# Emptying finished PSUM groups with ScalarE copies instead of VectorE adds in a four-layer attention kernel

## The chip, the cores and the metric

The kernel runs on one core of one Trainium2 chip. The time is the device time of one launch in microseconds (us), the median of several runs. The profile is one execution of the same program, recorded by the hardware profiler; its engines are called PE (TensorE's matmuls), PEld (TensorE's weight loads), DVE (VectorE), ACT (ScalarE), POOL (GpSimd) and SP (SyncE).

## What is computed

The input `x` is 4 images of 64 x 64 positions with 64 channels, fp32. Four layers follow one another:

- layer 0: self-attention over the 4096 positions of an image, `x = gamma * out + x`
- layer 1: layer norm, a 1x1 product to 256 channels, a depthwise 3x3 convolution, a gate, a 1x1 product back; then a second gated pair of 1x1 products; each added to `x`
- layer 2: attention without weights, in which the same memory is read as `B, C, H, W`
- layer 3: attention with 32 channels, a 1x1 product, then a normalization over all four images, added to `x`

What matters here is layer 2. In the reference it is

```
scores = jnp.einsum('bci,bcj->bij', xf, xf)
attn = jax.nn.softmax(scores, axis=-1)
out = jnp.einsum('bcj,bij->bci', xf, attn).reshape(B, C, H, W)
return out + x
```

with 4096 x 4096 scores per image. Because they are symmetric, the kernel computes only a part of the blocks and uses some exponentials twice, once as they are and once transposed.

## The kernel before, in words

**Order of the work.** Everything is unrolled at build time into a list of items; the instruction order on PE, ACT, DVE and POOL is the program's own order (`manual_schedule`), and each engine works through its own queue in that order. Only SP's queue (DMAs) is ordered by the tool. An item of layer 0 is a tile of 128 rows, one of layer 2 a block of 256 keys against 512 queries, one of layer 3 a tile of 128 keys. All images go through layer 0 first (items of image 0, 1, 2, 3), then layer 2 of image 0, then for each later image its layer 2 followed by layer 3 of the image before it, and last the layer 3 of image 3. Smaller work is woven in by two lanes, `conv` (layer 1 of an image, written as a generator that says how many nominal microseconds each step takes) and `misc` (projections, transposed inputs), which are advanced by `tick` in each item. `conv` carries layer 1 of image 3 during layer 2 of image 0. That puts the depthwise convolution (L1240 and L1243 on DVE, its first tap L1236 on ACT for image 3) and the writes of its padded input (L1222 on ACT, from the 1x1 products L1205) between the instructions of image 0's layer 2. `features2` (L1307 on PE, L1310 half on DVE and half on ACT) makes the transposed input `ko` of image 1 in the same stretch, in the `misc` lane.

**Layer 2 of one image.** A list of steps `(h, g, u, run, ti)` is built: `h` is one of 8 groups of 512 queries, `g` and `u` choose 256 keys. `item(n)` issues, in this order, the scores of step n (`score`, L1380, 8 matmuls into one of three 1024-wide PSUM slots, then two exps of 128x512, L1385, into an `e` tile), for mirrored steps the transposition of the exps (`turned`, L1398 on DVE) and their column sums (`column_sums`, L1413 by DMA for image 0, L1415 on POOL for the others, L1417 at the end of a group), then in image 0 a piece of `conv` and of `misc`, and last the products of the step two before (`products`, L1439, 8 matmuls). Products of one group accumulate in two PSUM banks, 6 and 7 (`new_acc`), one per row half `r`; each is a 128x512 tile. There is one such pair, so the first product of the next group can't start before both banks have been read. Image 0's groups are worked in the order 0, 1, 2, 3, 4, 7, 6, 5 (108 steps), the others' in the order 7, 0, 1, ..., 6 (72 steps).

**The sum array.** The result of a group, and what the transposed exps add to other groups, is gathered in an SBUF tile `m.A` (128x4096, 512 columns per group). It is allocated at step 2 of the image and cleared by POOL (L1478). At a group's last product two DVE adds (L1431, through `add_to`) add the two banks to its columns. `turned_products` (L1456, 128 small matmuls, 3.64 us) makes the contribution of a pair of mirrored blocks in two PSUM slots, and four adds of 128x256 (L1431 too) put it into the columns of the two groups of the pair. `spread_sums` (L1425 and L1426 on DVE) turns a group's column sums once POOL has finished them; for the last mirrored group it is issued after item `len(items) + 3` (image 0) or `+ 1` (the others). `close2` reads `m.A` and the sums (L1507, L1527) in the next image's items: its first part comes at item 8.

**Buffers.** `e` tiles (128x2048) come from a pool of six (`new_e`); a pair of steps shares one. In image 0 one of the six holds `xr`, the weights of the turned products, and one at a time holds `esum`. `A` comes from a pool of five large tiles.

Of the kernel before, what the change touches and what calls it, by code (L numbers as in the profile page):

```python
# [691 lines left out]
def fast_path(ctx: ExitStack, tc: tile.TileContext, a: dict, out: bass.AP, bad):  # L692
    nc = tc.nc
# [19 lines left out]
    PS = pp.tile([128, 4096], F32, name="PS")  # L713
# [12 lines left out]
    def new_ps():  # L726
        if turn_of["banks"]:
            if turn_of["bank"] % turn_of["banks"] == turn_of["banks"] - 1:
                turn_of["bank"] += 1
            k = new_bank(), new_bank()  # L730
            return PS[:, 512 * k[0] : 512 * k[0] + 1024]
        s = turn_of["slots"][turn_of["ps"] % len(turn_of["slots"])]
        turn_of["ps"] += 1
        return PS[:, bass.ts(s, 1024)]
# [9 lines left out]
    def new_acc():  # L744
        turn_of["acc"] += 1
        return PS[:, bass.ts(6 + turn_of["acc"] % 2, 512)]

    def new_e(name="e"):
        return ep.tile([128, 2048], F32, tag="e", name=name)
# [4 lines left out]
    def new_big(name):  # L754
        return big.tile([128, 4096], F32, tag="big", name=name)
# [78 lines left out]
    for nm in names128:  # L834
        r = flat[nm].shape[0] // 128
# [154 lines left out]
    items, due = [], {}  # L990

    def at(i, fn):
        due.setdefault(i, []).append(fn)
# [87 lines left out]
    def follow(lag=LAG):  # L1081
        if len(late) > lag:
            late.pop(0)()
# [238 lines left out]
    def layer2(b, when_free=None):  # L1322


        x, m, first = X[:, b], im[b], len(items)
# [14 lines left out]
        m.mirrored = [h for h, _ in (PART if b == 0 else FULL) if mine_t[h]]  # L1340
        spread_at = {mine_t[h][-1] + 5: h for h in m.mirrored}
        late_start, tiles = (6, 1) if b == 0 else (4, 2)
        used, todo = {}, []
        st = {"e": {}, "T": {}, "esum": {}}

        def slot(g, t):
# [4 lines left out]
        def weights(h):  # L1351
            if "xr" not in st:
                st["xr"] = new_e("xr") if b == 0 else xn.tile([128, 2048], F32, tag="xn", name="xn")
            for q in range(4):
                for k in range(4):
                    c = 1024 * (h % 2) + 256 * k
                    nc.sync.dma_start(  # L1357
                        out=st["xr"][32 * q : 32 * q + 32, c : c + 256],
                        in_=x[32 * k : 32 * k + 32, 256 * h : 256 * h + 256],
                    )  # L1360
# [6 lines left out]
        def score(n):  # L1367
            h, g, u, _, _ = steps[n]
            if n == 0:
                if b:  # L1370
                    take_slots(0, 1, 2)
                m.zs = sm.tile([128, 216], F32, tag="zs2", name="zs2")
            if n % 2 == 0:
                st["pair"] = new_e()
            e = st["e"][n] = st["pair"][:, bass.ts(n % 2, 1024)]
            ps = new_ps()
            for r, c in quads:
                rows_ = slice(64 * r, 64 * r + 64)
                k = 512 * g + 256 * u + 128 * r + 64 * c
                mm(  # L1380
                    ps[64 * c : 64 * c + 64, bass.ts(r, 512)], m.ko[rows_, k : k + 64],
                    m.ko[rows_, bass.ts(h, 512)], start=True, stop=True,
                )
            for r in range(2):
                act(  # L1385
                    e[:, bass.ts(r, 512)], ps[:, bass.ts(r, 512)], AF.Exp, bias=SHIFT2,
                    accum_out=slot(g, 2 * u + r),
                )

        def turned(n):  # L1390
            _, _, _, run, ti = steps[n]
            if run is None:
                return
            k = run % tiles
            if k not in st["T"]:
                st["T"][k] = new_big("turned")
            T = st["T"][k].rearrange("p (e s j) -> p s e j", e=16, s=8)
            nc.vector.transpose(  # L1398
                T[:, 2 * ti : 2 * ti + 2], st["e"][n].rearrange("p (s e i) -> p s e i", s=2, e=16)
            )  # L1400

        def column_sums(n):
            h, _, _, run, _ = steps[n]
            if run is None:
                return
            k, e = mine_t[h].index(n), st["e"][n]
            if k == (0 if b == 0 else 1):
                st["esum"][h] = new_e("esum")
            if h not in st["esum"]:
                return  # L1410
            esum = st["esum"][h][:, 0:1024]
            if b == 0:
                nc.gpsimd.dma_start(out=esum, in_=e, **({} if k == 0 else {"accum_op": ALU.add}))  # L1413
            else:
                nc.gpsimd.tensor_add(esum, st["e"][mine_t[h][0]] if k == 1 else esum, e)  # L1415
            if n == mine_t[h][-1]:
                nc.gpsimd.tensor_add(esum[:, 0:512], esum[:, 0:512], esum[:, 512:1024])  # L1417

        def spread_sums(h):
            if h == m.mirrored[0]:  # L1420
                m.cs = sm.tile([128, 128], F32, tag="cs2", name="cs2", bufs=1)
                if b == 0:
                    nc.gpsimd.memset(m.cs, 0.0)
            esum = st["esum"][h]
            nc.vector.transpose(esum[:, 512:1024], esum[:, 0:512])  # L1425
            nc.vector.tensor_reduce(  # L1426
                m.cs[:, bass.ts(h, 16)], esum[:, 512:1024].rearrange("p (e j) -> p e j", j=32), AX.X, ALU.add
            )

        def add_to(cols, ps):  # L1430
            nc.vector.tensor_add(cols, ps, cols)  # L1431

        def products(n):
            h, g, u, _, _ = steps[n]
            if n == mine[h][0]:
                st["acc"] = new_acc(), new_acc()
            for r, c in quads:
                rows_ = slice(64 * r, 64 * r + 64)
                mm(  # L1439
                    st["acc"][r][64 * c : 64 * c + 64, :], xw[rows_, 4 * g + 2 * u + c, :],  # L1440
                    st["e"][n][rows_, bass.ts(c, 512)], start=n == mine[h][0], stop=n == mine[h][-1],
                )
            if n == mine[h][-1]:
                for r in range(2):
                    add_to(m.A[:, bass.ts(h, 512)], st["acc"][r])

        def turned_products(run):
            h, pair, _ = runs[run]
            T, slots = st["T"][run % tiles], [new_ps(), new_ps()]
            for e in range(16):  # L1450
                c = e % 2
                w = 1024 * (h % 2) + 256 * (e % 4) + 64 * (e // 4)
                for q in range(4):
                    rows_ = slice(32 * q, 32 * q + 32)
                    o = 512 * (q % 2)
                    mm(  # L1456
                        slots[q // 2][64 * c : 64 * c + 64, o : o + 256], st["xr"][rows_, w : w + 64],
                        T[rows_, bass.ts(e, 256)], start=e < 2, stop=e >= 14,
                    )
            view = m.A.rearrange("p (g t q j) -> p g q t j", g=8, t=4, q=4)  # L1460
            for i in range(2):
                for gi, g in enumerate(pair):
                    add_to(
                        view[:, g, 2 * i : 2 * i + 2],
                        slots[i].rearrange("p (q m) -> p q m", q=2)[:, :, 128 * gi : 128 * gi + 128]
                        .rearrange("p q (t j) -> p q t j", j=32),
                    )

        def item(n):
            if n in weights_at:  # L1470
                weights(weights_at[n])
            score(n)
            turned(n)
            column_sums(n)
            todo.append(n)
            if n == 2:
                m.A = new_big("A")
                nc.gpsimd.memset(m.A, 0.0)  # L1478
            if b == 0:
                follow(0)  # L1480
                conv.tick(2.9)
                misc.tick(1.8)
            if n >= late_start:
                for _ in range(2):
                    if todo and todo[0] <= n - 2:
                        products(todo.pop(0))
            for run, (_, _, last) in enumerate(runs):
                if n - 2 == last:
                    turned_products(run)
                    if run == len(runs) - 2 and when_free:  # L1490
                        when_free()
            if n in spread_at:
                spread_sums(spread_at[n])

        for n in range(len(steps)):
            items.append((lambda n=n: item(n), 1.6 if b else 0.0))
        at(len(items), lambda: [products(todo.pop(0)) for _ in range(2)])
        for n, h in spread_at.items():
            if n >= len(steps):
                at(len(items) + (1 if b else 3), lambda h=h: spread_sums(h))  # L1500

    def close2(b):
        x, m = X[:, b], im[b]
# [525 lines left out]
```

## Time and profile before

| | |
|---|---|
| three runs | 2481.69, 2482.59, 2482.92 us; median 2482.59 |
| the profiled execution | 2481.6 us, of it 2479.7 between its first and last instruction (the span) |
| TensorE busy | 2428.8 us, 98% of the span |
| ScalarE busy | 1651.6 us, 67% |
| VectorE busy | 1466.9 us, 59% |
| GpSimd busy | 534.1 us, 22% |
| mean granted TensorE clock | 0.995 |
| layer 2 of image 0 | about 1019 to 1284 us from the span's start |
| layer 2 of images 1, 2, 3 | from about 1283, 1620 and 1957 us |
| group ends on VectorE (L1431, 128x512) | 64 adds, 686 ns mean |
| turned contributions (L1431, 128x256) | 188 adds, 417 ns mean |
| clearing of A (L1478, GpSimd) | 4, at 1023.5, 1292.1, 1608.6 and 1944.4 us, 3.5 to 3.8 us each |

A row of the profile's tables names a line of the code, the engine, the operation, and `out<-in` with the tile names; a time line row begins with its start and length in us and ends, in brackets, with the idle time of its engine before it and what ended it. A row with `xN` merges N neighbouring instructions. A row of the waits names engine, tile and line that waited, then `<-` what it waited for, the total in us, the number of times and the longest. A row of the windows gives a stretch, its length, then busy time (and instructions) of PE, PEld, DVE, ACT and POOL, the clock granted to TensorE (1.00 is full), the share of DMA time and GB/s.

### The profile page before, as it was taken

The page shows a single profiled execution, that of the slowest core. Times are in us where ns is not written, and L with a number is a line of the kernel's source. Part 1 is how long each engine was busy: PE and PEld are TensorE (multiplying, and loading weights), DVE is VectorE, ACT ScalarE, POOL GpSimd, SP SyncE. Part 2 cuts the span into 40 slices and gives each one's busy share as a digit, 9 for nine tenths or more (in the row PEclk, how much of TensorE's full clock was granted, in tenths as well). Part 3 has the DMA queues.
Part 4 walks back from the last instruction along what each step waited for, and adds up shares of the span by engine and source line. Part 5 has one row for each costly group of instructions (what it writes and reads, how often), then busy time and mean ns, then how long its engine had stood idle before and what let it go on. Part 6 is the DMA issues. An engine that isn't in the chain of part 4 may idle for free.

```text
span 2479.7 us, 63372 instructions
## 1 busy us (share of the span) xinstructions
PE 2428.8 (98%) x27381; PEld 932.6 (38%) x27381; DVE 1466.9 (59%) x1778; ACT 1651.6 (67%) x3162; POOL 534.1 (22%) x374
## 2 busy tenths in 40 slices
PE   9999999999999999989999999999999999999997
PEld 3343453336433633344334442134431244421113
DVE  2010377227822782377446657877668876678886
ACT  4666766676666666667744449954479754579996
POOL 2000000000000000100026662247631365622110
PEclk9999999999999999999999999999999999999999
DMA  3000000000000000320240017610065400296554
GB/s 79 1 18 1 18 1 18 18 19 1 18 18 18 1 18 18 65 48 18 52 86 19 19 45 154 135 29 19 19 130 121 92 19 19 61 173 141 120 118 117
DMA packets 65172, 129.57 MB, mean 52 GB/s; under 512 B 12556, under 2 KB 33269, under 8 KB 64885
## 3 DMA queue, kind: packets, MB, share of 16 engines
q0 software_dynamic: 22592, 80.26, 16.2%
q1 hardware_dynamic: 41541, 43.33, 7.7%
q8 instruction: 217, 3.56, 0.6%
q10 hardware_dynamic: 752, 1.85, 0.2%
q14 instruction: 70, 0.57, 0.1%
HBM read 4.80 MB, written 4.19 MB: 4 GB/s over the span
## 4 chain that ended last, share of the span: by engine, by line
PE 87%; DVE 6%; ACT 4%; issue 1%; SPq 1%; DMA 0%; POOL 0%; DVEq 0%; ACTq 0%
PE PS L1121 17%; PE PS L1095 17%; PE PS L1380 10%; PE PS L1439 10%; PE PS L1612 9%; PE PS L1673 8%; PE PS L1456 7%; DVE tg L1664 2%; PE PS L1205 2%; ACT e L1623 1%; DVE y L1240 1%; ACT e L1385 1%; SPq L1357 1%; ACT e L1100 1%; PE PS L1170 1%
## 5 line engine op out<-in xcount | busy, mean ns | idle before, releaser
L1100 ACT ACTIVATE e<-PS 128x1024 f32<-128x1024 f32 x512 | 524.2, 1024 | 333.1 <-PE PS L1095 300.1
L1385 ACT ACTIVATE e<-PS 128x512 f32<-128x512 f32 x648 | 380.7, 595 | 380.2 <-PE PS L1380 361.7
L1121 PE MATMUL PS<-e,vq 64*64 64x512 f32 x4096 | 577.2, 592 | 0.0
L1095 PE MATMUL PS<-X,q 64*64 64x512 f32 x4096 | 575.1, 591 | 1.8 <-DVE X L979 1.7
L1623 ACT ACTIVATE e<-PS 128x512 f32<-128x512 f32 (+2 forms) x588 | 500.4, 921 | 60.8 <-PE PS L1612 40.1
L1664 DVE TENSOR_TENSOR tg<-tg,e 128x2048 f32<-128x2048 f32 x172 | 393.9, 2290 | 42.6 <-ACT e L1623 31.0
L1439 PE MATMUL PS<-e,X 64*64 64x512 f32 x2592 | 373.6, 597 | 16.5 <-DVE A L1431 15.7
L1380 PE MATMUL PS<-ko 64*64 64x512 f32 x2592 | 376.1, 600 | 2.2 <-DVE A L1431 1.5
L1240 DVE SCALAR_TENSOR_TENSOR y<-pad,vec,y 128x1024 f32<-128x1024 f32 x240 | 308.0, 1283 | 29.8 <-ACT y L1236 22.4
L1415 POOL TENSOR_TENSOR esum<-esum,e 128x1024 f32<-128x1024 f32 x126 | 298.8, 2371 | 58.2 <-ACT e L1385 51.3
L1612 PE MATMUL PS<-tg,ph 32*64 32x512 f32 x4096 | 296.8, 612 | 2.6 <-DVE A L1431 1.8
L1398 DVE STREAM_TRANSPOSE turned<-e 128x1024 f32<-128x1024 f32 x188 | 231.4, 1239 | 112.5 <-ACT e L1385 112.5
L1095 PEld LDWEIGHTS PS<-X,q 64*64 64x64 f32 x4096 | 184.1, 133 | 258.8 <-issue 178.6
L1121 PEld LDWEIGHTS PS<-e,vq 64*64 64x64 f32 x4096 | 184.1, 133 | 252.2 <-issue 157.2
L1673 PE MATMUL PS<-e,tg 128*32 128x512 f32 x2048 | 272.5, 604 | 0.0
L1478 POOL MEMSET A<- 128x4096 f32 x4 | 14.7, 3675 | 1006.8 <-PE PS L1121 1006.8
L1439 PEld LDWEIGHTS PS<-e,X 64*64 64x64 f32 x2592 | 111.9, 134 | 198.9 <-issue 166.4
L1108 DVE TENSOR_REDUCE sums<-zs 128x1 f32<-128x4 f32 x128 | 19.7, 154 | 270.0 <-ACT e L1100 269.7
L1431 DVE TENSOR_TENSOR A<-PS,A 128x256 f32<-128x256 f32 (+1 forms) x252 | 110.5, 486 | 112.2 <-PE PS L1456 91.2
L1380 PEld LDWEIGHTS PS<-ko 64*64 64x64 f32 x2592 | 105.5, 133 | 167.4 <-issue 142.2
L1645 POOL DMA_DIRECT2D xn<-e x116 | 101.1, 898 | 291.2 <-ACT e L1623 208.0
L1456 PE MATMUL PS<-turned,xn 32*64 32x256 f32 x5376 | 157.9, 377 | 2.3 <-DVE sums L1519 1.4
(213 smaller groups left out, 1630.4 us busy)
## 6 DMA issues: line engine op xcount, KB each, us to landing
xn<-e POOLq DMA_DIRECT2D x132, 512.0 KB, 5.4
xn<-X SPq DMA_DIRECT2D x336, 32.0 KB
esum<-e POOLq DMA_DIRECT2D x20, 512.0 KB, 4.9
xn<-t SPq DMA_DIRECT2D x64, 128.0 KB
ph<-tg SPq DMA_DIRECT2D x64, 128.0 KB
ko<-ko SPq DMA_DIRECT2D x32, 128.0 KB
xr<-in_x_dram SPq DMA_DIRECT2D x13, 256.0 KB
q<-q SPq DMA_DIRECT2D x12, 256.0 KB
```

What stands on the lines that cost most here:

```text
L1095: mm(ps[64 * c : 64 * c + 64, bass.ts(r, 512)], m.q[rows_, 128 * t + 64 * c : 128 * t + 64 * c + 64], x[rows_, bass.ts(g, 512)], start=Tru ...
L1100: act(es[g // 2][:, bass.ts(g % 2, 1024)], ps, AF.Exp, bias=SHIFT0, accum_out=zs[:, g : g + 1],)
L1121: ins = mm(PS[64 * s : 64 * s + 64, 2048 + 512 * j : 2560 + 512 * j], vq[rows_, :], es[j // 2][rows_, k : k + 512], start=t == 0 and i < 2 ...
L1240: stt(y1, win, wt, y1, ALU.mult, ALU.add)
L1380: mm(ps[64 * c : 64 * c + 64, bass.ts(r, 512)], m.ko[rows_, k : k + 64], m.ko[rows_, bass.ts(h, 512)], start=True, stop=True,)
L1385: act(e[:, bass.ts(r, 512)], ps[:, bass.ts(r, 512)], AF.Exp, bias=SHIFT2, accum_out=slot(g, 2 * u + r),)
L1439: mm(st["acc"][r][64 * c : 64 * c + 64, :], xw[rows_, 4 * g + 2 * u + c, :], st["e"][n][rows_, bass.ts(c, 512)], start=n == mine[h][0], st ...
L1456: mm(slots[q // 2][64 * c : 64 * c + 64, o : o + 256], st["xr"][rows_, w : w + 64], T[rows_, bass.ts(e, 256)], start=e < 2, stop=e >= 14,)
L1612: mm(PS[64 * c : 64 * c + 64, bass.ts(banks[k], 512)], m.ph[32 * k : 32 * k + 32, 128 * mc + 64 * c : 128 * mc + 64 * c + 64], m.th[32 * k ...
L1623: act(e[:, 512 * lo : 512 * k], PS[:, 512 * banks[lo] : 512 * banks[lo] + 512 * (k - lo)], AF.Exp,)
L1664: nc.vector.tensor_add(esum, esum, e)
L1673: mm(st["y"][32 * k : 32 * k + 32, :], m.gx[:, i % 32, :], es[i][:, bass.ts(k, 512)], start=mc == 0, stop=i % 32 == 31,)
```

## The change

`add_to` is gone. A set `seen` records, for each image and while the program is built, which groups already have a contribution in `A`.

- At a group's end, if its columns have nothing yet, ScalarE copies the first bank (128x512) into them and VectorE adds the second.
- Otherwise, in image 0 only, ScalarE copies both banks with one instruction (128x1024) into a new `e` tile `own`, and VectorE makes the two adds from there. In the other images VectorE adds from PSUM as before.
- A turned contribution to columns that have nothing yet is a VectorE copy instead of an add.
- `A` is not cleared by GpSimd.
- The last mirrored group's `spread_sums` of image 0 is issued after item `len(items) + 6` instead of `+ 3`.

In image 0 groups 0, 7, 6 and 5 have nothing before their own end, groups 1 to 4 have. In the other images that holds for groups 7 and 0, while the later ones have turned contributions first.

```diff
-        used, todo = {}, []
+        used, todo, seen = {}, [], set()
...
-        def add_to(cols, ps):
-            nc.vector.tensor_add(cols, ps, cols)
-
...
             if n == mine[h][-1]:
-                for r in range(2):
-                    add_to(m.A[:, bass.ts(h, 512)], st["acc"][r])
+                got, cols = list(st["acc"]), m.A[:, bass.ts(h, 512)]
+                if h not in seen:
+                    seen.add(h)
+                    nc.scalar.copy(cols, got.pop(0))
+                elif b == 0:
+                    own = new_e("own")
+                    nc.scalar.copy(own[:, 0:1024], PS[:, 3072:4096])
+                    got = [own[:, 0:512], own[:, 512:1024]]
+                for acc in got:
+                    nc.vector.tensor_add(cols, acc, cols)
...
-                    add_to(
-                        view[:, g, 2 * i : 2 * i + 2],
+                    cols = view[:, g, 2 * i : 2 * i + 2]
+                    part = (
                         slots[i].rearrange("p (q m) -> p q m", q=2)[:, :, 128 * gi : 128 * gi + 128]
-                        .rearrange("p q (t j) -> p q t j", j=32),
+                        .rearrange("p q (t j) -> p q t j", j=32)
                     )
+                    if g in seen:
+                        nc.vector.tensor_add(cols, part, cols)
+                    else:
+                        nc.vector.tensor_copy(cols, part)
+            seen.update(pair)
...
                 m.A = new_big("A")
-                nc.gpsimd.memset(m.A, 0.0)
...
-                at(len(items) + (1 if b else 3), lambda h=h: spread_sums(h))
+                at(len(items) + (1 if b else 6), lambda h=h: spread_sums(h))
```

## The prediction

> **What bounds the kernel now.** I read the page's chain first, then TensorE's waits by window, then that part of the time line on every engine.
>
> ```profile
> PE 87%; DVE 6%; ACT 4%; issue 1%; SPq 1%; DMA 0%; POOL 0%; DVEq 0%; ACTq 0%
> ...
> 1019.00:1292.00 273.00, 257.61 (x2698) 108.79 (x2693) 154.78 (x177) 179.07 (x504) 23.84 (x25) 0.98 0.29 60
> ...
> PE PS L1439 <- DVE A L1431: 15.7, 5, 5.1
> PE PS L1380 <- DVE A L1431: 1.5, 1, 1.5
> ```
>
> TensorE is the chain; only its idle time can be won. Image 0's layer 2 (second line; PE is the first number after the length) leaves 15.4 us idle. TensorE's own waits, taken from 1019 to 1310 us, name the cause: five times the first product of a new group (L1439) waits for VectorE's adds (L1431), 15.7 us in all. Four lie in image 0, one at image 1's start.
>
> ```profile
> 1086.40 1.23 PE L1439 MATMUL PS<-e,X 64*64 64x512 f32 x8
> 1087.25 1.23 PE L1380 MATMUL PS<-ko 64*64 64x512 f32 x8
> 1093.59 2.68 PE L1439 MATMUL PS<-e,X 64*64 64x512 f32 x8 [5.11 <-DVE A L1431]
> 1095.33 2.65 PE L1380 MATMUL PS<-ko 64*64 64x512 f32 x8
> ...
> 1082.20 9.20 DVE L1240 SCALAR_TENSOR_TENSOR y<-pad,vec,y 128x1024 f32<-128x1024 f32 x7
> 1091.43 1.42 DVE L1243 SCALAR_TENSOR_TENSOR yg<-pad,vec,y 128x512 f32<-128x512 f32 x2
> 1092.76 1.48 DVE L1431 TENSOR_TENSOR A<-PS,A 128x512 f32<-128x512 f32 x2
> ...
> 1087.96 1.24 ACT L1236 ACTIVATE y<-pad,vec 128x1024 f32<-128x1024 f32 x1
> 1089.10 0.59 ACT L1385 ACTIVATE e<-PS 128x512 f32<-128x512 f32 x1
> ```
>
> Columns are start and length. Group 1's last products start at 1086.40 and the adds at 1092.76, because image 3's depthwise convolution stands ahead of them on VectorE. ScalarE sits almost idle meanwhile (no exp between 1090.3 and 1098.0). A block of eight matmuls normally starts 0.86 us after the last; after the stall the blocks start 1.74, 1.70 and 1.27 us apart: half clock, 2.13 us more.
>
> ```profile
> 1292.07 3.50 POOL L1478 MEMSET A<- 128x4096 f32 x1
> ...
> 1292.15 0.71 DVE L1425 STREAM_TRANSPOSE esum<-esum 128x512 f32<-128x512 f32 x1 [4.39 <-POOL esum L1417]
> ...
> 1295.61 1.49 DVE L1431 TENSOR_TENSOR A<-PS,A 128x512 f32<-128x512 f32 x2 [0.87 <-POOL A L1478]
> 1296.36 4.48 PE L1439 MATMUL PS<-e,X 64*64 64x512 f32 x16 [4.15 <-DVE A L1431]
> ```
>
> At image 1's start GpSimd's clearing of A runs late, behind the last column sum, and VectorE waits for both.
>
> Cost now, as delay of the next block against the 0.86 pitch, plus half clock read from the blocks after it: group 1 1088.11 to 1093.59, 5.5 + 2.1; group 2 3.5 + 0; group 3 1.5 + 0; group 4 2.2 + 1.7; image 1 4.3 + 3.2 (blocks 3.46 for two, 1.71, 1.42). Sum 24.0 us: the ceiling there.
>
> **What the Trainium skill says.** "TensorE: Matmul & The Clock Gate", What's actually happening: an idle window of about 3.4 us, free-running, halves the clock until a busy window has passed. The trace agrees in kind (2.13 us lost after 5.11 idle) and in the looseness: 2.98 us idle cost nothing at 1116.4, 2.05 cost 1.7 at 1169.3. So I can't say which remaining gap goes cold. The same page (table at its head) has ScalarE and VectorE as strict FIFO; the trace shows it: adds whose operands are complete stand behind the convolution. "VectorE: DVE Perf Modes", Why PSUM operands drop a tier: fp32 from PSUM runs at the base rate. Agreed: a 128x256 copy from PSUM is 425 ns (L941), the add 417 (L1431).
>
> **The change part by part.**
> Groups 1 to 4 of image 0: four ScalarE copies of 128x1024 (1016 ns, L1970's copy from PSUM) now free both banks; eight VectorE adds read SBUF, not shown here in this place; bounds 693 ns (L1276, same shape) and 991 (L1534, strided); I take 0.69, as both operands are contiguous, so VectorE's load stays (686 before).
> - Group 1: the copy is queued after that item's exps and the L1236 that starts 1087.96, so 1089.1 to 1090.2; TensorE resumes at 1090.25 instead of 1093.59, 3.3 + 2.1 saved: 5.5. Behind the copy on ScalarE stand the next exps, 1 us later; products need them two steps on, so that is covered.
> - Group 2: exps end 1112.94 in today's times, copy to 1113.98, resume 1114.05 instead of 1116.41: 2.4. Running 7.8.
> - Given back: ScalarE's pad writes for the convolution's other half (L1222, 1122.30 now) must wait until VectorE has read the old pad, today 1121.03. VectorE can only come earlier by its 4.28 us wait for L1236 at 1109: done 1116.8, so ScalarE is 5.5 us earlier, not 7.8. Its exps are behind it; TensorE has 0.5 us of slack in score buffers. Running 5.9.
> - Group 3: copy instead of add, 1.3 saved: 7.2. Then ScalarE's half of image 1's transposed copy (L1310) waits for VectorE's half behind adds and convolution (already 3.29 us now); VectorE is still 5.5 early, TensorE's slack 1.0 (the score block at 1147.57 reuses the buffer that L1310 leaves at 1146.54), so back to 6.2.
> - Group 4: copy behind the exps ending 1166.75, to 1167.8: resume about 1.0 us after pitch instead of 2.2, half clock gone: 2.9. Running 9.1. The later wait, L1260 for the channel sum at 1193.9, has VectorE 8.3 early and 2 us of slack: not late.
> First contributions: image 0's groups 0, 7, 6, 5 and two per later image: one 587 ns copy (L1679's, the same shape) on ScalarE, then one add instead of two. At group 7 TensorE's second row half gets its bank at 1202.6 instead of 1203.2: 0.3. The others lie beside a turned run (3.64 us of TensorE) or already show no delay.
> Turned runs: first ones copy instead of add, 0.425 against 0.417: nothing.
> Memsets: four of 3.5 to 3.8 us leave GpSimd. Images 2 and 3 had them at 1608.6 and 1944.4 with GpSimd next busy at 1636: nothing. Image 1, with the column spreading of group 5 moved three items later (two VectorE instructions, 1.4 us, no DMA; its reader L1507 comes at item 8): exps of item 4 end 1292.05, copy to 1292.65; VectorE transposes item 4's block to 1293.35 and adds the second half by 1294.05. The block starts about 1.9 us late instead of 4.3, saving 2.4 + 3.2 = 5.5 (both rounded). If A's buffer came free late, ScalarE would wait there with exps behind it; GpSimd's own waits for it ended by 1290.9.
> Images 2 and 3: two adds at 1631.48 after a 1.25 us transpose hold TensorE until 1632.98; copy plus one add end by 1632.2, and L1708 behind them comes 0.7 earlier: 0.7 each, 1.4.
> Remaining gaps of 2.1, 1.9, 1.9 (pads), 1.2 and 1.0 us may go cold: bounds 0 and three times 2; I take one, -2.0.
> **Sum:** 9.1 + 0.3 + 5.5 + 1.4 - 2.0 = 14.3 us. The profiled execution took 2481.6 us (span 2479.7 and 1.9 around it), so 2467.3 of its kind; it lies 1.0 under the median 2482.6, so 2468.3.
>
> **Rivals.** About 0.2%, 5 us, is what a measurement of this kernel tells from no change.
> - Mostly moved: VectorE's convolution chain stays the bound, pads and L1310 return nearly all of groups 1 to 4 and two gaps go cold. For: VectorE is 14.5 of 15 us busy at 1086 to 1101. Against: its 4.28 and 2.83 us waits for L1236 are TensorE's delay and close. Left 5.5 + 1.4 - 1 = 6: 2477. Chance 0.15.
> - Nearly all of it: no give-back, no cold gap: 14.3 + 2.0 + 2.9 + 1 = 20: 2462. Chance 0.13.
> - Slower: the copied group takes one of six e buffers. If the very next pair of exps gets that buffer, they wait at the head of ScalarE's queue for the two VectorE adds (copy end 1090.2 to add end 1094.1, 3.9 us), with L1236, which VectorE needs, behind them. Each end then costs 3.9 + 2.1 cold; 24 for four, plus 4.1 of copies and 4.7 of first copies now in the chain, less 16.5 (today's four) and 6.9 won elsewhere: +9.4, 2492. It decides once reuse comes within two steps; xr, at most three live pairs and this one make five of six, which speaks against. Chance 0.07.
> - The copies don't free the banks sooner, because ScalarE is late by as much as VectorE: no gain, 2482. ScalarE's idle after 1090 speaks against. Chance 0.05.
> The forecast itself has 0.60.
>
> **How the numbers follow.** Best-case 2462 and the six-us case 2477 bound the main uncertainties (cold gaps 0 to 6 us; adds 0.69 or 0.99, 2.4 us; give-back). Range 2461 to 2477. Faster by over 0.2%: 0.60 + 0.13 and over half of 0.15, 0.82; within, the rest of it and the last rival, 0.11; slower 0.07.
>
> **What would show it.** TensorE's waits for L1431's successor in 1019 to 1310 fall from 15.7 to under 6 us, none above 2.5; clock in 1086 to 1101 back from 0.77; ScalarE idle before its pad writes at about 1114; GpSimd without L1478; image 1's first group gap near 2. Wrong if ScalarE's exps wait for VectorE's adds after a group end, or the waits at pads and L1310 exceed 5 us.

## The result and the profile after

| | before | after |
|---|---|---|
| median, beside each other | 2482.14 us (2480.24 to 2482.92, 4 runs) | 2461.96 us (2460.21 to 2464.22, 4 runs) |
| the profiled execution: its span | 2479.7 us | 2458.3 us |
| TensorE busy | 2428.8 us | 2418.3 us |
| mean granted TensorE clock | 0.995 | 0.998 |

The ratio is 0.992, with a 95% interval of 0.9903 to 0.9938: 20.2 us less. The forecast was 14.3; 20 is the number of the rival "nearly all of it". The median lies 1 us inside the forecast's range of 2461 to 2477. Profiled again later, the changed kernel had a median of 2459.73 us, below that range, and a ratio of 0.991 (0.9894 to 0.9925). In the changed kernel the products are L1436 (L1439 before), the first-contribution copy is L1444, the copy of both banks L1447, the adds L1450, the turned contributions L1474 and L1476; lines from L1507 on moved by 9.

TensorE is still the chain (87% of the span, as before); only what it waits for has changed. The windows of the kernel after (length; busy time and instructions of PE, PEld, DVE, ACT, POOL; clock; DMA share; GB/s):

```profile
1019.00:1280.00 261.00, 251.98 (x2702) 92.96 (x2700) 153.82 (x176) 186.47 (x518) 20.54 (x25) 1.00 0.31 63
1086.00:1101.00 15.00, 13.32 (x124) 4.49 (x120) 14.64 (x14) 11.37 (x32) 0.00 (x0) 1.00 0.00 1
1276.00:1290.00 14.00, 13.51 (x124) 4.17 (x124) 8.64 (x15) 8.89 (x29) 9.10 (x5) 1.00 0.09 23
```

Image 0's layer 2 is 12 us shorter and leaves TensorE 9.0 us idle instead of 15.4. The second row is the end of group 1 and the third the start of image 1; before, the clock was 0.77 in both places (1086 to 1101 and 1290 to 1305 us), and after it is full. At group 1 ScalarE has more to do (11.4 us busy; 6.4 in the same 15 us before), while VectorE is as full as it was. TensorE's own waits from 1019 to 1310 us in the kernel after:

```profile
PE PS L1436 <- ACT own L1447: 2.9, 3, 1.7
...
PE PS L1292 <- DVE u L1288: 1.3, 1, 1.3
PE PS L1380 <- ACT ko L1310: 1.1, 1, 1.1
...
PE PS L1307 <- ACT ko L1310: 0.5, 2, 0.3
PE PS L1436 <- DVE A L1450: 0.3, 1, 0.3
PE PS L1436 <- ACT A L1444: 0.2, 1, 0.2
```

The 15.7 us of products waiting for VectorE's adds became 3.4 us (2.9 + 0.3 + 0.2), none over 1.7. New in the list is `ko`. The end of group 1 in the kernel after, TensorE and then ScalarE:

```profile
1086.21 1.04 PE L1436 MATMUL PS<-e,X 64*64 64x512 f32 x8
1087.07 1.04 PE L1380 MATMUL PS<-ko 64*64 64x512 f32 x8
1089.79 1.09 PE L1436 MATMUL PS<-e,X 64*64 64x512 f32 x8 [1.68 <-ACT own L1447]
1090.70 1.04 PE L1380 MATMUL PS<-ko 64*64 64x512 f32 x8
...
1087.60 1.24 ACT L1236 ACTIVATE y<-pad,vec 128x1024 f32<-128x1024 f32 x1
1088.73 1.00 ACT L1447 COPY own<-PS 128x1024 f32<-128x1024 f32 x1
```

The copy stands behind L1236 on ScalarE, as the prediction said, and the next group's products start 2.7 us after the scores instead of 6.3. The blocks behind them are 0.86 to 0.91 us apart: no half clock.

To compare executions I cut TensorE's time at four instructions that every kernel has: the last products of group 1 (1086.40 before), the channel sum L1260, the last L1292, and the first matmul of `close2` (L1507 before) for image 0 and for image 3. That takes out the up to 1.7 us by which executions differ ahead of the first cut. A difference of 0.2 in the first column says nothing: the four quarters of the array (64x64 tiles) that share a block of eight matmuls can run up to 0.2 us apart at the cut, and 0.5 in spread3. Lengths in us:

| kernel | group 1 to L1260 | to the last L1292 | to the close | to image 3's close |
|---|---|---|---|---|
| before | 107.52 | 78.75 | 34.21 | 863.37 |
| after | 94.55 | 78.22 | 28.09 | 861.89 |
| after, again | 94.54 | 77.76 | 28.09 | 861.88 |
| own_only | 94.76 | 83.79 | 30.17 | 863.30 |
| no_own | 109.54 | 81.83 | 28.26 | 861.95 |
| memset_kept | 94.77 | 78.01 | 32.25 | 861.91 |
| dve_first | 94.75 | 83.55 | 29.05 | 863.60 |
| own_only_late | 94.75 | 78.37 | 33.15 | 863.32 |
| pads_rev | 97.66 | 78.41 | 28.10 | 861.93 |
| ko_act | 92.45 | 78.55 | 28.09 | 861.91 |
| best (two copies) | 92.64 | 76.82 | 28.09 | 861.87 |
| best_whole | 92.45 | 76.82 | 28.09 | 861.90 |
| best_first | 91.64 | 76.81 | 28.09 | 861.89 |
| spread3 | 95.05 | 78.41 | 28.80 | 861.70 |

The change won 13.0 us at groups 1 to 4, 0.5 up to the last L1292, 6.1 at image 1's start and 1.5 at images 2 and 3: 21.1 of the 21.4 between the two spans.

### The profile page after: what moved, and what is told of

Same layout as the page of the kernel before. It is cut to its first block, busy times and chain, and to the rows that moved or that the text cites. A ratio compares the mean times of both kernels' runs of the same rounds, so it can differ in the third digit from the quotient of the medians.

```text
span 2458.3 us, 63365 instructions
## 1 busy us (share of the span) xinstructions
PE 2418.3 (98%) x27381; PEld 917.1 (37%) x27381; DVE 1459.6 (59%) x1768; ACT 1659.2 (67%) x3176; POOL 520.6 (21%) x370
## 4 chain that ended last, share of the span: by engine, by line
PE 87%; DVE 5%; ACT 5%; issue 1%; DMA 1%; SPq 0%; POOL 0%; ACTq 0%; DVEq 0%; POOLq 0%
PE PS L1121 18%; PE PS L1095 18%; PE PS L1380 10%; PE PS L1436 10%; PE PS L1621 9%; PE PS L1682 8%; PE PS L1461 7%; PE PS L1205 2%; DVE tg L1673 2%; ACT e L1632 2%; ACT e L1385 1%; DMA xn<-e 1%; ACT e L1100 1%; PE PS L1170 1%; PE PS L1063 1%
## 5 line engine op out<-in xcount | busy, mean ns | idle before, releaser
L1380 PE MATMUL PS<-ko 64*64 64x512 f32 x2592 | 348.7, 596 | 3.3 <-DVE A L1474 1.5
L1436 PE MATMUL PS<-e,X 64*64 64x512 f32 x2592 | 343.6, 591 | 4.0 <-ACT own L1447 2.9
L1240 DVE SCALAR_TENSOR_TENSOR y<-pad,vec,y 128x1024 f32<-128x1024 f32 x240 | 308.0, 1283 | 18.2 <-ACT y L1236 10.8
L1413 POOL DMA_DIRECT2D esum<-e x20 | 16.5, 825 | 1227.8 <-ACT e L1385 1188.5
L1436 PEld LDWEIGHTS PS<-e,X 64*64 64x64 f32 x2592 | 101.1, 133 | 185.3 <-issue 160.1
L1380 PEld LDWEIGHTS PS<-ko 64*64 64x64 f32 x2592 | 94.9, 132 | 173.3 <-issue 149.1
L1621 PEld LDWEIGHTS PS<-tg,ph 32*64 32x64 f32 x4096 | 64.2, 129 | 223.3 <-ACT e L1632 184.7
```

The costliest lines, as they stand in the source:

```text
L1240: stt(y1, win, wt, y1, ALU.mult, ALU.add)
L1380: mm(ps[64 * c : 64 * c + 64, bass.ts(r, 512)], m.ko[rows_, k : k + 64], m.ko[rows_, bass.ts(h, 512)], start=True, stop=True,)
L1436: mm(st["acc"][r][64 * c : 64 * c + 64, :], xw[rows_, 4 * g + 2 * u + c, :], st["e"][n][rows_, bass.ts(c, 512)], start=n == mine[h][0], st ...
L1621: mm(PS[64 * c : 64 * c + 64, bass.ts(banks[k], 512)], m.ph[32 * k : 32 * k + 32, 128 * mc + 64 * c : 128 * mc + 64 * c + 64], m.th[32 * k ...
```

## Experiments

The theory: each stall was its own, and each part of the change removes its own. The rivals are written into the expectations. own_only, no_own, dve_first and memset_kept ran beside a kernel before of 2482.41 us; own_only_late, pads_rev, ko_act and best beside one of 2481.53.

**own_only**: the kernel before, with the ScalarE copy at groups 1 to 4 alone.

```diff
-                for r in range(2):
-                    add_to(m.A[:, bass.ts(h, 512)], st["acc"][r])
+                got, cols = list(st["acc"]), m.A[:, bass.ts(h, 512)]
+                if b == 0 and h in (1, 2, 3, 4):
+                    own = new_e("own")
+                    nc.scalar.copy(own[:, 0:1024], PS[:, 3072:4096])
+                    got = [own[:, 0:512], own[:, 512:1024]]
+                for acc in got:
+                    add_to(cols, acc)
```

> The kernel before with one part of the change: ScalarE's 128x1024 copy at the ends of image 0's groups 1 to 4; A is still cleared, first contributions are still added. Theory (each stall is its own, and what is won stays won): 5.7 + 3.5 + 2.3 - 2.0 + 3.5 = 13.0 us less, about 2469. TensorE's three gaps at groups 1 to 4 and the half clock at 1086 to 1101 are gone, the 4 us gap and the half clock at image 1's start stay. Rival (absorbed): GpSimd's column sum and clearing at image 1's start end when they ended before, so TensorE waits there for all that it is early, and the time is within 2 us of the kernel before, 2482.

Measured: 2474.26 us, ratio 0.9962 (0.9948 to 0.9976). 8 us, not 13. The first column of the table shows that the copies did their whole work (12.8 us); but 5.0 us went again between L1260 and the last L1292, a place neither theory had named. VectorE there in own_only, then the matmul that waits:

```profile
1226.88 0.71 DVE L1425 STREAM_TRANSPOSE esum<-esum 128x512 f32<-128x512 f32 x1 [7.45 <-POOL esum L1417]
...
1228.22 1.27 DVE L1288 SCALAR_TENSOR_TENSOR u<-PS,pwb,t 128x1024 f32<-128x1024 f32 x1
...
1229.56 1.98 PE L1292 MATMUL PS<-u,pw 128*64 128x512 f32 x4 [4.08 <-DVE u L1288]
```

L1288, which TensorE needs, stands behind a spreading (L1425) that waits for GpSimd's column sum. TensorE idles 4.1 us and then runs at half clock (1.98 us for a group of 1.08). In the kernel after the wait is 1.3 us, because the sum is ready at 1223.2 instead of 1226.9. GpSimd's issues of the accumulating column-sum DMAs, and SP's norm DMAs, in own_only:

```profile
1201.28 0.61 POOL L1413 DMA_DIRECT2D esum<-e  x1 [120.18 <-ACT e L1385]
1205.70 0.86 POOL L1413 DMA_DIRECT2D esum<-e  x1 [3.81 <-ACT t L1179]
1213.86 0.88 POOL L1413 DMA_DIRECT2D esum<-e  x1 [7.30 <-DMA esum<-e]
...
1205.24 9.18 SPq L1183 DMA_DIRECT2D xn<-t  x8
```

and in the kernel after:

```profile
1200.38 0.60 POOL L1413 DMA_DIRECT2D esum<-e  x1 [119.91 <-ACT e L1385]
1203.87 0.86 POOL L1413 DMA_DIRECT2D esum<-e  x1 [2.88 <-ACT t L1178]
1209.62 0.88 POOL L1413 DMA_DIRECT2D esum<-e  x1 [4.90 <-ACT e L1385]
...
1204.35 10.04 SPq L1183 DMA_DIRECT2D xn<-t  x8
```

After, the second column sum is issued 0.5 us ahead of SP's eight transfers and is no hindrance to the third; in own_only it is issued 0.5 us behind them, and the third waits for it until 1213.9. "DMA: Bandwidth & Descriptors" of the Trainium skill, Issuing engines are not separate DMA queues, says that DMAs of different engines share the same 16 DMA engines and interleave; the trace agrees: the same 512 KB were done 5.2 us after issue in one kernel and 7.6 in the other. What put it behind is the first transfer, which took 3.9 us in own_only against 3.0 after: SP's transfers start 4.0 us after the first issue in both. The DMA view of own_only from 1201 to 1205 us has, beside the transfer's 144 packets,

```profile
q14 instruction: 1, 0.01, 1.0%
```

and that of the kernel after, in the same place, has no such row. One instruction fetch fell into the first transfer in own_only, no_own, dve_first and own_only_late (3.5 to 3.9 us long), and in those four the second issue came 0.1 to 0.5 us behind SP's; in the ten others none did, the first transfer took 2.9 to 3.0 us, and the second issue came 0.5 us ahead. That is an association in fourteen profiles; nothing was run that moves a fetch by itself, and what places it stays open. Of own_only's six runs one took 2467.32 us, the others 2472 to 2477.

**own_only_late**: the same, with VectorE's spreading one item later.

```diff
-        spread_at = {mine_t[h][-1] + 5: h for h in m.mirrored}
+        spread_at = {mine_t[h][-1] + (5 if b else 6): h for h in m.mirrored}
```

> The kernel with only ScalarE's copies for groups 1 to 4 of image 0, and VectorE's spreading of image 0's column sums issued one item later, so that it stands behind L1288 instead of ahead of it on VectorE. Theory: the 5 us that the copies alone fell short of (2474 instead of 2469) went at 1225 to 1231, where L1288 stood on VectorE behind a spreading that waited for a late column sum; that wait of TensorE (4.1 us, with half clock) is gone and the time is about 2469, with less scatter. Rival: the column sum is late for all, and the wait only moves to the next reader; 2473 or more.

Measured: 2465.78 us, ratio 0.9936 (0.9924 to 0.9948). VectorE and TensorE in own_only_late:

```profile
1221.52 1.28 DVE L1288 SCALAR_TENSOR_TENSOR u<-PS,pwb,t 128x1024 f32<-128x1024 f32 x1 [3.56 <-PE PS L1205]
1225.55 0.71 DVE L1425 STREAM_TRANSPOSE esum<-esum 128x512 f32<-128x512 f32 x1 [2.74 <-POOL esum L1417]
...
1224.74 1.08 PE L1292 MATMUL PS<-u,pw 128*64 128x512 f32 x4
```

The column sum was late again (its third issue came at 1213.0), and TensorE didn't notice. So the shortfall was a late sum ahead of L1288 in VectorE's queue. The time is 3 us below the theory's 2469; the table shows 1.1 of that at image 1's start and 0.4 ahead of the last L1292, and leaves the rest open. This is a place that the prediction never looked at, since its wait in the kernel before is 1.0 us; the changed kernel met no more than 1.3 us there.

**no_own**: the changed kernel without the `elif b == 0` branch (four lines taken out).

> The changed kernel without the branch that copies both banks with ScalarE: groups 1 to 4 of image 0 are added from PSUM by VectorE again; first contributions stay copied, A stays uncleared. Theory: image 1's start 6.0, images 2 and 3 1.6, group 7 0.3: 8 us less than the kernel before, about 2474; the gaps of groups 1 to 4 are back (5.1 us at group 1, half clock behind it). Rival (absorbed): TensorE's start of image 1 is set by what is late there in either case, and this part alone brings nearly all of the gain, 2464 or less.

Measured: 2478.52 us, ratio 0.998 (0.9971 to 0.9989). The last two columns are the changed kernel's: image 1's start and images 2 and 3 are won without the copies, 7.4 us. The stalls of groups 1 to 4 are back, with the clock at 0.77 (1086 to 1101 us) and 0.87 (1165 to 1178), and cost 2.0 more than before in this execution: group 2's gap has the same 2.98 us as before, but here the clock fell behind it (the last section shows why). The late column sum costs 3.1. Absorption holds in neither kernel: the copies' 12.8 us were not lost at image 1's start, and this part alone doesn't bring the whole gain.

**dve_first**: the first bank copied by VectorE.

```diff
-                    nc.scalar.copy(cols, got.pop(0))
+                    nc.vector.tensor_copy(cols, got.pop(0))
```

> The changed kernel with the first bank of a group without a contribution copied by VectorE instead of ScalarE; A stays uncleared. Theory: the absent clearing and the moved transposition do most of image 1's 6 us; ScalarE's sharing is worth 0.7 at each of images 1, 2 and 3 and 0.3 at group 7: about 2 more than the changed kernel, 2464. Rival: it is ScalarE's copy that lifts image 1's start, and half or more of the 6 us is lost with it, 2466 or more.

Measured: 2469.14 us, ratio 0.9945 (0.9932 to 0.9958). By the total the rival seems right, but the table says otherwise: image 1's start costs 1.0 more than in the changed kernel and images 2 and 3 1.7, which is the theory's size; 5.3 us lie in the column with the late sum.

**memset_kept**: the changed kernel with GpSimd's clearing of A kept.

```diff
                 m.A = new_big("A")
+                nc.gpsimd.memset(m.A, 0.0)
```

> The changed kernel with GpSimd's clearing of A kept at its old place; nothing else differs, and what it clears is overwritten by the first copies. Theory: at image 1 the clearing runs late behind the last column sum, ScalarE's first copy waits for it, and the gap of 4 us with its half clock is back: about 2468 (5 to 6 more than the changed kernel); at images 2 and 3 nothing. Rival: the clearing wasn't the last thing waited for (VectorE's transposition behind the column sum was), so the time stays within 1.5 us of the changed kernel, 2462.

Measured: 2464.47 us, ratio 0.9924 (0.9912 to 0.9937). ScalarE's copy at image 1's start in memset_kept:

```profile
1281.24 0.59 ACT L1444 COPY A<-PS 128x512 f32<-128x512 f32 x1 [3.08 <-POOL A L1488]
```

The mechanism is the theory's (a 3.4 us wait of TensorE behind the clearing, clock 0.83 from 1280 to 1290 us, 4.2 us in the third column), its size a little less than the 5 to 6 expected. This rests on the trace: by its interval the median can't be told from the changed kernel's.

**pads_rev**: the changed kernel with the pad's pieces of the second half written in the order 3, 2, 1, 0.

```diff
-            for j in range(4):
+            for j in ((3, 2, 1, 0) if b == B - 1 and not r else range(4)):
```

> The changed kernel with the four pieces of the padded input of image 3's second convolution half written in the order 3, 2, 1, 0. Theory: in the order 0 to 3 the first pieces touch no row that VectorE's last convolution block still reads, so ScalarE needn't wait; in this order piece 3 must wait until VectorE has finished that block (1116.1 in the changed kernel, where piece 0 starts at 1112.7), ScalarE stands 3 us with its exps behind it, and TensorE loses 2 to 3 us there, after its 0.5 us of slack: about 2464.5, with a wait behind L1222 or its exps. Rival: the prediction's give-back was absent for another reason (VectorE had been won enough), so the order of the pieces is nothing: within 1 us of the changed kernel.

Measured: 2463.03 us, ratio 0.993 (0.9916 to 0.9944); the table has it 3.1 us behind the changed kernel, all in the first column: 2.5 at the pads, the rest at L1310, where TensorE waits 1.7 us instead of 1.1. The medians alone (2463.03 and 2461.96) don't show it. In the kernel after, ScalarE's first piece starts while VectorE is still in the old half:

```profile
1112.67 1.42 ACT L1222 ACTIVATE pad<-PS,pwb 128x512 f32<-128x512 f32 x2
...
1114.68 1.42 DVE L1243 SCALAR_TENSOR_TENSOR yg<-pad,vec,y 128x512 f32<-128x512 f32 x2
```

and ScalarE's wait in pads_rev is the one that the prediction had feared:

```profile
ACT pad L1222 <- DVE yg L1243: 3.4, 1, 3.4
```

Counted in the padded input, L1222's piece j covers rows 8j+1 to 8j+8 and 8j+33 to 8j+40, and VectorE's last block reads rows 48 to 65. Piece 0 touches none of those. Piece 1 touches row 48 alone; the last of the nine taps that reads it, the seventh (L1240), was done at 1113.3 us, before piece 1 started at 1115.2. Piece 3 touches rows 57 to 64, which the last tap (L1243) still reads.

**ko_act**: both halves of L1310 for image 1 on ScalarE.

```diff
-            for e, copy in enumerate((nc.vector.tensor_copy, nc.scalar.copy)):
+            for e, copy in enumerate((nc.scalar.copy if b == 1 else nc.vector.tensor_copy, nc.scalar.copy)):
```

> The changed kernel with both halves of image 1's transposed copy (L1310) on ScalarE. Theory: TensorE's 2.0 us lost between 1135 and 1145 come from ScalarE waiting for VectorE's half behind the convolution; with no VectorE half, TensorE's waits for ko (1.1 + 0.5 us) go and the time is 2 less than the changed kernel's, 2460. Rival: four more copies of 0.58 us on ScalarE delay the exps by as much: no gain, 2462 or more.

Measured: 2458.35 us, ratio 0.991 (0.9896 to 0.9924). The first column is 2.1 us shorter and TensorE's waits for `ko` are gone. The give-back at L1310 is real and is 2 us. This too rests on the trace: the intervals of the two kernels overlap.

**best, best_whole, best_first**: `ko_act`'s and `own_only_late`'s edits on the changed kernel; "best" also copies the two banks in two instructions, best_first instead issues a group's last products and copy ahead of that item's `conv` and `misc` steps. The last two ran beside the changed kernel (2459.73 us) and a before of 2481.76 us.

The first three lines are best's, the last four best_first's:

```diff
-                    nc.scalar.copy(own[:, 0:1024], PS[:, 3072:4096])
+                    for r in range(2):
+                        nc.scalar.copy(own[:, bass.ts(r, 512)], got[r])
...
+            if b == 0 and todo[0] <= n - 2 and todo[0] in [mine[h][-1] for h in (1, 2, 3, 4)]:
+                products(todo.pop(0))
             if b == 0:
                 follow(0)
```

> The changed kernel with three additions: both halves of L1310 for image 1 on ScalarE, the two banks of groups 1 to 4 copied by ScalarE in two instructions of 128x512 instead of one of 128x1024, and image 0's spreading one item later. Theory: 2.0 from ko, 0.4 at each of three waits for the copy (1.2, as the next product needs only the first bank), 1.3 from L1288 no longer behind the spreading: 4.5 less than the changed kernel, about 2457.5. Rival: TensorE's waits return at the next buffer (exps behind two copies and four ko halves): 2461 or more.

> The changed kernel itself, unaltered, beside the next kernels on one chip. All theories: 2462, within 2.

> The changed kernel with both halves of L1310 for image 1 on ScalarE and image 0's spreading one item later; the two banks are copied with one instruction, as in the changed kernel. Theory: copying the banks in two instructions brought nothing, since the two row halves of a product run side by side and the one that waits for the second bank ends no sooner; so this is within 0.7 us of the version with two instructions, about 2456. Rival: the halves were worth 1.2 us: about 2457.

> The kernel of the run before with one more edit: at the ends of groups 1 to 4 of image 0 the last products and the copy are issued ahead of that item's convolution and misc steps instead of behind them. Theory: at group 1 the copy no longer stands behind L1236 (1.13 us) on ScalarE, and TensorE's wait of 1.7 us there falls to about 0.6: 1.1 less. Rival: the convolution's first tap, now 1 us later, makes VectorE late and the pads or the next conv block give it back: no gain or slower.

Measured: best 2455.81 us (ratio 0.9898, 0.9881 to 0.9914), best_whole 2457.52 (0.9903, 0.9888 to 0.9918), best_first 2455.61 (0.9896, 0.988 to 0.9912). The intervals overlap with each other and with the changed kernel's (0.9894 to 0.9925), so the order among them rests on the trace: from group 1 to image 3's close best_first is 3.8 us shorter than the changed kernel beside it, best_whole 3.0, and best no more than best_whole. best_first took TensorE's wait at group 1 from 1.7 to 0.5 us and won 0.8 by it. Two copies lowered TensorE's waits for the copy from 2.8 to 1.3 us in the list and won nothing. TensorE behind group 1 in best shows why:

```profile
1088.93 0.64 PE L1436 MATMUL PS<-e,X 64*64 64x512 f32 x1 [1.25 <-ACT own L1448]
...
1089.42 0.65 PE L1436 MATMUL PS<-e,X 64*64 64x512 f32 x3
```

The eight matmuls, two for each quarter of the array, no longer run as one block: one quarter goes ahead when the first bank is free, and the other three start when the second is, at 1089.42 us (ScalarE's two copies, 1.07 us together, start at 1088.30). The last three products of the block start behind the first score. "TensorEngine Tiling (Array Packing)", Key Properties, says that different tiles of the array can work in parallel; the trace agrees. The pace is set by the later bank. (The expectation of best_whole speaks of two row halves; in the trace it is one quarter against three.)

**spread3**: the changed kernel with `+ 3` instead of `+ 6` for the last spreading.

> The changed kernel with the last spreading of image 0 issued after item len(items) + 3 again. Theory: VectorE then waits for the column sum (done at about 1277.6), spreads for 1.4, transposes for 1.2 and adds at about 1280.1 instead of 1279.3: TensorE's second bank comes 0.8 later, 0.8 more than the changed kernel. Rival: with 1.2 us of gap and more the clock falls to half and 3 us are lost.

Measured: 2461.66 us, ratio 0.9917 (0.9904 to 0.9931). The third column is 0.7 us longer, as the theory says; no half clock. (Its first column is no loss: the quarters ran 0.5 us apart at the cut, and from the next group's first product to L1260 it took 90.96 us, the changed kernel 90.97.) By the median alone it can't be told from the changed kernel.

## Why the prediction was right, and where it was off

The mechanism was right: the stalls were VectorE's adds and GpSimd's clearing, and TensorE gained where ScalarE's copies or the absent clearing took them away. The range held the time, but by 1 us, and three terms were off in the same direction. The steps, in us; the measured ones are shifts between TensorE's instructions in the profiles of before and after, within a block of eight at the matmuls that start last:

| step | predicted | measured |
|---|---|---|
| group 1 | 5.5 | 5.9 |
| group 2 | 2.4 | 3.1 |
| pads, given back | -1.9 | 0 |
| group 3 | 1.3 | 2.3 |
| L1310, given back | -1.0 | -2.0 |
| group 4 | 2.9 | 3.5 |
| group 7 | 0.3 | 0.3 |
| image 1's start | 5.5 | 6.0 |
| images 2 and 3 | 1.4 | 1.6 |
| one gap at half clock | -2.0 | 0 |

(The expectation of own_only has 5.7 and 3.5 for groups 1 and 2, which mixes first and last matmuls of a block.)

**Pads.** "Must wait until VectorE has read the old pad" is the step that failed. It took the tile as one thing to wait for; the writes wait for the rows they touch. In the order of the code the first two pieces are free by the time they are written, and pads_rev shows that the forecast's wait comes with the other order.

**Groups 2, 3 and 4** were mis-sized because I counted the delay of the block's first matmul. TensorE at group 2's end in the kernel before:

```profile
1116.41 1.04 PE L1439 MATMUL PS<-e,X 64*64 64x512 f32 x2 [2.98 <-DVE A L1431]
1117.11 0.65 PE L1439 MATMUL PS<-e,X 64*64 64x512 f32 x3
...
1115.58 1.48 DVE L1431 TENSOR_TENSOR A<-PS,A 128x512 f32<-128x512 f32 x2
```

The two matmuls of one quarter of the array start at 1116.41 and 1116.86, when VectorE's first add has freed one bank; the other six start at 1117.11 and 1117.59, after the second add (686 ns mean). So "can't start before both banks have been read", as the kernel was described, holds for six matmuls of eight. The six come 0.8 us behind the first at group 3 and 0.7 at group 4. One copy frees both banks at once. These three steps were too small by 0.7, 1.0 and 0.6 us, about the length of that second add. "best" is the same effect from the other side.

**L1310** was foreseen in kind. TensorE came 11.6 us earlier to it, VectorE's first half only 9.5 (1135.8 instead of 1145.3), and nearly all of the difference was given back. 1.3 of the 2.0 went at the score block that the prediction named, where its slack of 1.0 was there. (Its own numbers, 7.2 less 5.5 less 1.0, make 0.7 and not the 1.0 that it took.) The other 0.7 went at the third and fourth piece of the transposed input, where TensorE's L1307 waits for ScalarE's L1310; the prediction did not count those. ko_act measures the whole: 2.1.

**Half clock.** I charged one gap of those left. None went cold; the longest left is 1.7 us. The -2.0 stood for one of three gaps, taken without a reason, between bounds of 0 and -6, and the upper bound was right. The last section shows what the prediction could not say, which gaps go cold.

**Image 1** fell as worked out: the absent clearing is 4.2 us of it (memset_kept), ScalarE's share 1.0 (dve_first), the moved spreading 0.7 (spread3). These three make 5.9 of the 6.1, though parts undone one at a time need not add up.

The rival "slower by reuse of e buffers" had no place: no wait of ScalarE for an add of L1450 shows after a group end; its exps follow the copy at once (1089.62 after the copy that starts at 1088.73). "Copies free the banks no sooner" fell at group 1, where TensorE resumed 3.8 us sooner (1089.79 instead of 1093.59). "Mostly moved" fell with the pads. "Nearly all of it" has the measured number, partly by luck: no gap went cold and the pads gave nothing back, as it says, but L1310 gave back 2.0, and the steps that I had taken too small made up for that. Without the pads' and the half clock's terms my own sum would have been 18.2 us. The measured steps add up to 20.7, and the undersized groups, 2.7 us in all, are more than the difference; L1310 took 1.0 of that back.

## What to carry to other kernels

When an accumulator pair is emptied by an engine that has a long queue, count the delay by the later bank, not by the first matmul that resumes. Before you charge a give-back to a buffer, compare the rows that the writer and the last reader touch, and the order in which the pieces are written. An instruction that waits for a DMA-fed sum should not stand ahead of one that TensorE needs: half a microsecond in the order of two DMA issues went with 5 us here, and moving two instructions back on VectorE took that away.

## What the runs showed of the hardware that I had not expected

Whether a gap is followed by half clock is not told by its length between 2 and 3.4 us: 2.05 (group 4 before), 2.98 (group 2 in no_own), 3.04 (own_only_late, image 1) and 3.36 us (memset_kept) were, 2.83 (own_only, image 1) and 2.98 us (group 2 before) were not. At image 1's start that alone is the 3.0 us between own_only and own_only_late in the third column. What tells it is where the gap lies. In the kernel before, the half-clock stretches of image 0's layer 2 start at 1091.02, 1169.53 and 1295.82 us and last 6.83, 3.41 and 6.83 us: lengths and distances (78.51 and 126.29) are whole multiples of 3.413 us, and the same holds within each of the other profiles. So the clock is decided once per window of 3.413 us, on a grid that doesn't move with the program. Group 2's gap of 2.98 us, first in the kernel before, then in no_own, by such windows (the first number after the length is TensorE's busy time, the eighth column the clock):

```profile
1111.50:1114.92 3.42, 1.93 (x19) 0.53 (x11) 3.31 (x4) 2.53 (x8) 0.00 (x0) 1.00 0.00 0
1114.92:1118.33 3.41, 1.92 (x14) 1.02 (x18) 3.27 (x5) 0.00 (x0) 0.00 (x0) 1.00 0.00 0
...
1113.55:1116.97 3.42, 1.59 (x10) 0.76 (x14) 3.32 (x4) 0.22 (x2) 0.00 (x0) 1.00 0.01 2
1116.97:1120.38 3.41, 3.41 (x20) 1.90 (x16) 2.95 (x4) 1.27 (x4) 0.00 (x0) 0.50 0.00 0
```

Before, the gap falls on two windows, 1.49 us idle in each, and the clock stays; in no_own 1.83 us of it fall into one window, and the next runs at half clock. Over the fourteen profiles between 1019 and 1310 us, the eleven windows after which the clock fell had 1.82 us of idle or more; of some 1170 other windows at full clock all but one had 1.68 or less (the one, in dve_first, had 1.92). A gap of up to 1.7 us, as they are left in the kernel after, is therefore safe in this stretch, and one between 1.8 and about 3.6 us (twice 1.82, an estimate) can go either way. It is no general bound: in layer 3, between 2213 and 2233 us, the clock fell three times after windows with 1.27 to 1.77 us of idle. The Trainium skill's account in "TensorE: Matmul & The Clock Gate", What's actually happening, has a free-running window of that length, and the trace agrees; but where it asks for an idle window of about 3.4 us, a window little more than half idle was enough here. And a fetch of instructions, one packet, coincided in four profiles of four with a 512 KB transfer of 3.5 to 3.9 us instead of 3.0.
